# Nested products for six of the seven products of q, v and k in a float32 attention and non-local block

## The chip, the cores and the metric

The kernel runs on one core of a Trainium2 chip. The metric is the device time of one execution in microseconds (us), lower is better. TensorE (PE) multiplies matrices, VectorE (DVE), ScalarE (ACT) and GpSimd (POOL) work element by element, SyncE (SP) issues most DMAs. All data is float32.

## The reference, cut to what matters

Eight images of 512 channels and 32 x 32 positions pass through two layers:

```
h, d = 8, 64                                  # 8 heads of 64 channels, n = 1024 positions
q, k, v = (conv1x1(x, W, b) for q, k and v)   # 512 -> 512 channels each
attn = softmax(einsum('bhdn,bhdm->bhnm', q, k) * d ** -0.5)
x = x + conv1x1(einsum('bhnm,bhdm->bhdn', attn, v), Wp, bp)

g, theta, phi = (conv1x1(x, w, b) for g, theta and phi)   # 512 -> 256 channels
f = einsum('bcn,bdn->bcd', theta, phi) / n
z = conv1x1(einsum('bcd,bdn->bcn', f, g), W_w, W_b) + x
out = batch_norm(z) over (image, position), times gamma, plus beta
```

The change concerns the three 512 x 512 by 512 x 1024 products that make q, k and v of each image.

## The kernel before, in words

The kernel goes through the images one after the other. For image b it has q, k and v already; it then does, in this order on TensorE: the attention of b (`attention`, 64 steps of scores, exponential and weighted sum); q, v and k of image b+1 (`heads_of`, `values`, `heads_of`), with the softmax denominators of b inside the q stage; the output projection (`project`); theta and phi (`theta_phi`); f, g and z (`nonlocal_`). The order of TensorE's instructions, and of those passed through `pe(...)`, `dve(...)` and `sp(...)`, is kept as written; the rest is placed by a scheduler, which also inserts the waits.

Every large product is made by a scheme of seven block products instead of eight (`SEVEN`, lines 235 to 238; a Strassen-Winograd form). The weight matrix is cut into 2 x 2 blocks of 256 x 256, the data into 2 x 2 blocks of 256 channels by 512 positions. Four sums of weight blocks (`weight_sums`) and four sums of data blocks (`t1` to `t4`, `more_sums`, L216) are formed; seven products are made in PSUM, and each is added to one or two quarters of the result: the first time by ScalarE with the bias (L410, L403, L429), later by VectorE (L346, L430). A block product is 4 matmuls of 128x512 for q and k (8 of 128x256 for v, whose result has positions on partitions).

For q, v and k three of the seven block products (`INNER`, numbers 1, 2 and 6) are made by the same scheme once more, from blocks of 128 x 128 and 128 x 256 (`nested`, L268 and L271): seven matmuls of 128x256 in place of four of 128x512, or fourteen of 128x128 in place of eight of 128x256. They need three more weight sums per product (kept in DRAM beside the weights) and four more data sums (`inner_parts`, L228). `seven` interleaves them with the four plain products by the tables `HALVES`, `STEPS` and `READS`; `fills` are calls that stand at given places in that order, for example sums for the next stages. The projection of images 1 to 6 has two nested products, all others are plain.

Buffers: a weight matrix with all its sums is one tile of 18.5 KB per partition in a pool of two (`wr`); `load_w` (L133) fetches the next one when a stage has ended. A ring of ten 4 KB tiles (`block`, pool `ring`) holds the exponentials and the data sums. PSUM is four slots of two banks, handed from stage to stage in the list `free`.

The softmax denominators: VectorE adds the exponentials of a unit (two heads, half the positions) in `acc` (L466, L468). At the unit's end `together` (L495 to L498) folds the 128 partitions of `acc` to 32: SyncE copies the first quarter, then three GpSimd-issued DMAs add the others, one after the other. In the q stage of the next image, at unit 14 of the interleaving, `all_denominators` makes their sum on TensorE (L525), VectorE takes the reciprocal (L536), and a DMA through DRAM spreads it over partitions (`r`, L582). GpSimd multiplies `o` by it in the v stage (`normalize`, L568, four products of 128x1024).

`near_end` (L884) forms the first data sums of the next image on VectorE at step 62 of 64 of the attention: two of 128x1024 and four of 128x256, ahead of the last sum into `acc`.

At the start, image 0's q, k and v are made with weights that arrive piece by piece (L356 to L369, L852 to L876). Image 0's v has three nested products, its q and k none. At the end, `last_z`, `begin` and `finish` (L818 to L846) form z of the last images, the mean and the variance, and write the output channel block by channel block; a check of the denominators (L986 to L990) stands beside it.

Of the kernel before, what the change touches and what calls it, by code (L numbers as in the profile page):

```python
# [16 lines left out]
P = 128  # L17
# [13 lines left out]
def unshifted(ctx: ExitStack, tc: tile.TileContext, a: dict, out: bass.AP):  # L31
# [19 lines left out]
    wr = ctx.enter_context(tc.tile_pool(name="wr", bufs=2))  # L51
    w3 = ctx.enter_context(tc.tile_pool(name="w3", bufs=3))
    foldp = ctx.enter_context(tc.tile_pool(name="foldp", bufs=1))
    ring = ctx.enter_context(tc.tile_pool(name="ring", bufs=10))
# [47 lines left out]
    def weight_sums(w, a21, which=(3, 4, 5, 6), pin=lambda ins: None):  # L102
        for to, l, r, op in ((3, a21, w[:, 2], ALU.add), (4, w[:, 3], w[:, 0], ALU.subtract),
                             (5, w[:, 0], a21, ALU.subtract), (6, w[:, 1], w[:, 4], ALU.subtract)):
            if to in which:
                pin(nc.vector.tensor_tensor(w[:, to], l, r, op))


    queue = ["WqT", "WkT", "WvT"]
    for b in range(B):  # L110
        queue += (["WqT", "WvT", "WkT"] if b < B - 1 else []) + ["WpT", "tp", "WgT"]
    loaded = []

    INNER = {"WqT": (1, 2, 6), "WkT": (1, 2, 6), "WvT": (1, 2, 6), "WpT": (1, 2)}
    WIDTH = 7 * C + 3 * 3 * P
    rest = {}

    def weights_tile(name, half):
        t = wr.tile([P, WIDTH], F32, tag="w", name=f"w_{name}")
        rest[name] = t[:, 14 * half:]  # L120
        return t, t[:, :14 * half].rearrange("p (i k f) -> p i k f", i=7, k=2)

    def load_w(dma, pin=lambda ins: None):

        if not queue:
            return
        name = queue.pop(0)
        half = quarter(name, 0, 0).shape[2]
        t, w = weights_tile(name, half)
        loaded.append((name, w))  # L130
        if name in kept:
            of = kept["plain"] if name == "WpT" and len(queue) == 2 else kept[name]
            ins = dma.dma_start(t[:, :of.shape[1]], of)  # L133
            pin(ins)
            if len(queue) == 1:
                sp(ins)
            return
        corner[name] = block(f"a21_{name}")[:, :, :half]
        for to, m, k in ((w[:, 0], 0, 0), (w[:, 1], 0, 1), (w[:, 2], 1, 1), (corner[name], 1, 0)):
            dma.dma_start(to, quarter(name, m, k))  # L140

    def weights(name, sums_done=False, pin=lambda ins: None):

        n, w = loaded.pop(0)
        assert n == name
        if name not in kept:
            if not sums_done:
                weight_sums(w, corner[name], pin=pin)
            if name not in ("WqT", "WkT", "WvT"):
                keep("plain" if name == "WpT" else name, w)  # L150
        return w

    def keep(name, w):
        kept[name] = dram.tile([P, 14 * w.shape[3]], F32, tag=f"kept_{name}", name=f"kept_{name}")
        nc.sync.dma_start(kept[name], w.rearrange("p i k f -> p (i k f)"))

    def inner_blocks(w, name, n):

        a = w[:, INNER[name][n]]
        extra = rest[name][:, n * 3 * P:(n + 1) * 3 * P].rearrange("p (i f) -> p i f", i=3)  # L160
        return [a[:, 0, :P], a[:, 1, :P], a[:, 1, P:], a[:, 0, P:], extra[:, 0], extra[:, 1], extra[:, 2]]

    def keep_inner(name, w):

        for n in range(len(INNER[name])):
            inner_weights(name, w, n)
        keep_all(name, w)

    def inner_weights(name, w, n):

        a11, a12, a22, a21, s2, s3, s4 = inner_blocks(w, name, n)
        for to, l, r, op in ((s3, a11, a21, ALU.subtract), (a21, a21, a22, ALU.add), (s2, a21, a11, ALU.subtract),
                             (s4, a12, s2, ALU.subtract)):
            dve(nc.vector.tensor_tensor(to, l, r, op))

    def keep_all(name, w):

        wide = len(INNER[name]) * 3 * P
        kept[name] = dram.tile([P, 14 * w.shape[3] + wide], F32, tag=f"kept_{name}", name=f"kept_{name}")
        nc.sync.dma_start(kept[name][:, :14 * w.shape[3]], w.rearrange("p i k f -> p (i k f)"))  # L180
        nc.sync.dma_start(kept[name][:, 14 * w.shape[3]:], rest[name][:, :wide])
# [49 lines left out]
    def quarters_of(t):  # L231
# [17 lines left out]
    FOUR = tuple((*one[:4], ()) for one in (SEVEN[0], SEVEN[1], SEVEN[2], FIVE[4]))  # L249
    HALVES = ((0, 0), (0, 1), (1, 0), (2, 0), (2, 1), (1, 1), (3, 0), (3, 1))  # L250
    STEPS = {2: [0] * 4 + [1] * 14, 3: [0, 0, 0, 1, 1, 2, 2, 2, 2, 2, 2, 2, 2, 1, 1, 1]}
    READS = {3: ((0, "11", True),), 9: ((0, "12", True),), 11: ((1, "22", True),), 13: ((1, "12", False),),
             15: ((0, "22", False), (0, "21", False))}

    def nested(name, stage, w, data, tags, first, add, positions_out=False):

        slots = [bank(tag, f"{name}_in_{tag}") for tag in tags]
        goes_to = {1: ("11", "21", False), 6: ("12", "22", False), 2: ("21", "t4", True)}
# [23 lines left out]
    def seven(name, w, data, positions_out, first, add, between=None, early=False,  # L282
# [19 lines left out]
        for n, m in HALVES if three else ((n, None) for n in range(len(products))):  # L302
# [16 lines left out]
            for i, (to_ps, at, lhsT, rhs, k) in enumerate(work):  # L319
# [3 lines left out]
                if three and positions_out and not i % 2:  # L323
                    continue
# [879 lines left out]
```

## Time and profile before

| | |
|---|---|
| time of the runs, median of 3 | 2135.36 us (2135.02 to 2135.43) |
| time of the profiled execution | 2134.36 us |
| its span, first to last instruction | 2132.6 us |
| granted TensorE clock, mean | 0.996 |
| TensorE busy | 2108.4 us, 99% |
| VectorE, ScalarE, GpSimd busy | 1390.1, 747.5, 210.3 us |
| HBM read and written | 146.23 and 46.86 MB |
| weights of one matrix, W_q with its sums | 2368 KB, 8.9 us from issue to landing |

The profile's page gives busy times by engine, groups of instructions by line and tile, and the chain of work that ended last, followed back from the last instruction: the engine and line that was late at each moment. Timelines list an engine's instructions with their start, their length, and in brackets the idle time ahead and what ended it. "L468" is a line of the kernel; "acc<-acc,e" are the tiles written and read.

One image takes 261.5 us. Counted from the start of the attention of image 1 (341.0), its parts begin at: q of image 2 451.1, v 475.3, k 498.5, projection 521.3, theta and phi 544.5, g 568.7, f 577.3, z 590.4, next attention 602.5.

### The profile page before, as it was taken

Reading aid. Unit: us, or ns where it says so; the run is one execution under the profiler, and the core shown is the slowest. Engines: PE = TensorE matmul, PEld = TensorE weight load, DVE = VectorE, ACT = ScalarE, POOL = GpSimd, SP = SyncE. Lnnn points to the kernel's source line nnn. Section 1 sums busy time; section 2 is a strip of 40 time slices with the busy share of each in tenths; the row PEclk is TensorE's granted clock in tenths of the full one; section 3 lists DMA queues with packets and bytes.
Section 4 is the critical chain, followed back from the end, with each engine's and each line's share of the span. In section 5 each row is a group of like instructions: output and inputs, shape, how many; then the busy total and the mean of one; then the engine's idle time right before and its main releaser. Section 6 shows DMA issues by size and latency. Waiting matters only on the chain.

```text
span 2132.6 us, 31250 instructions
## 1 busy us (share of the span) xinstructions
PE 2108.4 (99%) x13018; PEld 1124.3 (53%) x13018; DVE 1390.1 (65%) x1856; ACT 747.5 (35%) x873; POOL 210.3 (10%) x221
## 2 busy tenths in 40 slices
PE   9999999999999999999999999999999999999996
PEld 4534764357733567336673366633766347643462
DVE  6566667676576665766657667576674675656746
ACT  1464104641046310463105621066212652056116
POOL 0011100111001110011001120011200111011000
PEclk9999999999999999999999999999999999999998
DMA  6522544224142332423223242242434224122758
GB/s 209 193 41 35 155 160 139 40 36 155 73 142 40 52 135 77 142 40 72 112 111 112 40 102 94 101 107 41 104 129 173 38 39 131 58 55 40 227 200 343
DMA packets 53317, 228.75 MB, mean 107 GB/s; under 512 B 10672, under 2 KB 17328, under 8 KB 45616
## 3 DMA queue, kind: packets, MB, share of 16 engines
q1 hardware_dynamic: 42240, 200.33, 26.9%
q0 software_dynamic: 9072, 24.78, 9.6%
q8 instruction: 104, 1.70, 0.3%
q10 hardware_dynamic: 1856, 1.56, 0.3%
q14 instruction: 45, 0.37, 0.1%
HBM read 146.23 MB, written 46.86 MB: 91 GB/s over the span
## 4 chain that ended last, share of the span: by engine, by line
PE 97%; ACT 1%; DVE 1%; DMA 1%; issue 0%; SPq 0%; DVEq 0%; ACTq 0%
PE po L485 21%; PE ps L459 21%; PE ptp L320 9%; PE pp L320 7%; PE pq L320 6%; PE pk L320 6%; PE pv L320 5%; PE pg L320 4%; PE pv_in_s L268 3%; PE pk_in_s L271 3%; PE pq_in_s L271 3%; PE pz L320 3%; PE pf L670 2%; PE pp_in_s L271 2%; PE pwf L725 1%; ACT z L845 1%
## 5 line engine op out<-in xcount | busy, mean ns | idle before, releaser
L462 ACT ACTIVATE e<-ps 128x1024 f32<-128x1024 f32 x512 | 523.1, 1025 | 436.2 <-PE ps L459 430.0
L468 DVE TENSOR_TENSOR acc<-acc,e 128x1024 f32<-128x1024 f32 x384 | 470.1, 1224 | 145.1 <-ACT e L462 141.9
L459 PE MATMUL ps<-q,k 64*64 64x512 f32 x4096 | 529.6, 590 | 1.0 <-DVE v L430 1.0
L485 PE MATMUL po<-e,v 64*64 64x512 f32 x4096 | 528.7, 589 | 0.0
L485 PEld LDWEIGHTS po<-e,v 64*64 64x64 f32 x4096 | 156.6, 133 | 282.9 <-issue 275.4
L459 PEld LDWEIGHTS ps<-q,k 64*64 64x64 f32 x4096 | 155.4, 133 | 284.6 <-issue 273.4
L498 POOL DMA_DIRECT2D fold<-acc x189 | 144.7, 766 | 1613.8 <-PE ps L459 836.2
L713 ACT ACTIVATE g<-pg,gb 128x512 f32<-128x512 f32 x31 | 21.3, 687 | 475.6 <-PE pg L320 475.5
L466 DVE TENSOR_TENSOR acc<-e,e 128x1024 f32<-128x1024 f32 x64 | 78.3, 1224 | 132.5 <-ACT e L462 132.5
L430 DVE TENSOR_TENSOR v<-v,pv_in_s 128x256 f32<-128x256 f32 x136 | 56.8, 421 | 97.6 <-PE pv_in_s L268 79.4
L320 PE MATMUL ptp<-w_tp,t_x 128*128 128x256 f32 x512 | 114.4, 379 | 0.0
L320 PEld LDWEIGHTS ptp<-w_tp,t_x 128*128 128x128 f32 x512 | 97.3, 190 | 13.2
L320 PE MATMUL pp<-t_o,w_WpT 128*128 128x512 f32 x208 | 100.8, 592 | 0.0
L320 PE MATMUL pq<-t_x,w_WqT 128*128 128x512 f32 x200 | 100.6, 596 | 0.0
L320 PE MATMUL pk<-t_x,w_WkT 128*128 128x512 f32 x200 | 100.0, 592 | 0.0
L320 PE MATMUL pv<-w_WvT,t_x 128*128 128x256 f32 x384 | 98.8, 380 | 0.0
L320 PE MATMUL ptp<-w_tp,x 128*128 128x256 f32 x384 | 86.8, 379 | 0.0
L568 POOL TENSOR_TENSOR o<-o,r 128x1024 f32<-128x1024 f32 x28 | 65.4, 2354 | 153.7 <-DMA r<-den_d 131.5
L320 PEld LDWEIGHTS ptp<-w_tp,x 128*128 128x128 f32 x384 | 73.0, 190 | 13.3 <-issue 3.8
L346 DVE TENSOR_TENSOR k<-k,pk_in_s 128x256 f32<-128x256 f32 x119 | 48.0, 419 | 47.7 <-PE pk_in_s L271 35.1
L346 DVE TENSOR_TENSOR q<-q,pq_in_s 128x256 f32<-128x256 f32 x119 | 48.1, 416 | 45.1 <-PE pq_in_s L271 32.8
L320 PE MATMUL pp<-o,w_WpT 128*128 128x512 f32 x144 | 67.8, 593 | 1.6 <-DVE o L566 1.6
(200 smaller groups left out, 2349.1 us busy)
## 6 DMA issues: line engine op xcount, KB each, us to landing
fold<-acc POOLq DMA_DIRECT2D x189, 128.0 KB, 3.1
w_WqT<-kept_WqT SPq DMA_DIRECT2D x7, 2368.0 KB, 8.9
w_WvT<-kept_WvT SPq DMA_DIRECT2D x7, 2368.0 KB, 8.8
w_WkT<-kept_WkT SPq DMA_DIRECT2D x7, 2368.0 KB, 16.2
r<-den_d SPq DMA_DIRECT2D x32, 512.0 KB, 6.7
x<-in_x_dram SPq DMA_DIRECT2D x30, 512.0 KB, 5.9
w_WpT<-kept_WpT SPq DMA_DIRECT2D x6, 2176.0 KB, 8.1
w_tp<-kept_tp SPq DMA_DIRECT2D x7, 1792.0 KB, 7.2
```

The source lines that it names most:

```text
L268: pe(nc.tensor.matmul(ps[:, i, :], d[di][:, i * P:(i + 1) * P], a[wi], start=s not in begun and not i, stop=True, skip_group_check=True))
L271: pe(nc.tensor.matmul(ps, a[wi], d[di], start=s not in begun, stop=True, skip_group_check=True))
L320: pe(nc.tensor.matmul(to_ps, lhsT(k), rhs(k), start=(s, at) not in begun, stop=(k == nk - 1), skip_group_check=True))
L346: pin(nc.vector.tensor_tensor(at, at, ps if len(ps.shape) == 3 else ps.unsqueeze(1), ALU.add))
L430: lambda q, ps: dve(nc.vector.tensor_tensor(at(q), at(q), as_v(ps), ALU.add)), **how)
L459: pe(nc.tensor.matmul(ps[c * P // 2:(c + 1) * P // 2, j, :], k[r, p, keys], q[r, p, h * 512:(h + 1) * 512], start=True, stop=True, skip_gr ...
L462: nc.scalar.activation(e, ps, AF.Exp, scale=SCALE)
L466: nc.vector.tensor_tensor(accs[u], es[u, 0], e, ALU.add)
L468: ins = nc.vector.tensor_tensor(accs[u], accs[u], e, ALU.add)
L485: pe(nc.tensor.matmul(ps[j * D:(j + 1) * D, r, :], v[keys, m, (2 * p + j) * D:(2 * p + j + 1) * D], e[keys, j, :], start=(m == 0), stop=(m ...
L498: nc.gpsimd.dma_start(to, part_of, accum_op=ALU.add)
L568: dve(nc.gpsimd.tensor_tensor(at, at, of, ALU.mult))
```

## The change

Six of the seven block products of q, v and k are nested, for images 1 to 7; only the product of the blocks 11 stays plain. Image 0's q, k and v are all plain. A new function `six` takes them in three pairs, `SIX`, whose matmuls alternate, over all four PSUM slots. Products that go to several quarters are collected in three temporary tiles (T1, T6, T7 in the pool `w3`) and added to the quarters by GpSimd, for v partly by VectorE. The bias enters by T1 and, as a difference (`dq`, `dk`), by T7.

Weights are held by blocks: units of 7 KB per partition, two nested blocks with their sums each, in a pool of four (`wr`), and the plain first block in a pool of two (`wf0`). `load_w` fetches one unit after each pair. The ring has twelve tiles. To make room, `tpb` is loaded again for every image, `dens` lies in a ring tile that is loaded at the end, `f` in a ring tile, and the sums of `o` in the tile of `fold`. W_k of image 0 lies at first in the tiles of `o` and `fold`.

The denominators and the reciprocal stand at `"middle"`, between the second pair and the plain product of q. Two of the four products with `r` move from GpSimd to VectorE. The data sums of the next image, now four nested blocks more, are formed one by one at the steps `AT` of the attention (26 to 57).

The core of the diff (the rest of it renames, or follows from the blocks):

```diff
-    wr = ctx.enter_context(tc.tile_pool(name="wr", bufs=2))
+    wr = ctx.enter_context(tc.tile_pool(name="wr", bufs=4))
+    wf0 = ctx.enter_context(tc.tile_pool(name="wf0", bufs=2))
-    ring = ctx.enter_context(tc.tile_pool(name="ring", bufs=10))
+    ring = ctx.enter_context(tc.tile_pool(name="ring", bufs=12))
...
+    PAIRS = ((1, 6), (3, 4), (5, 2))
+    UNITS = {"WqT": PAIRS, "WkT": PAIRS, "WvT": PAIRS, "WpT": ((1, 2), (3, 4, 5), (6,)), "tp": ((3, 4, 2), (6, 5, 1)),
+             "WgT": (range(7),)}
...
+    SIX = (((1, "21", "11"), (6, "22", "12")), ((3, "t1", "22"), (4, "t2", "T6")), ((5, "t3", "T7"), (2, "t4", "21")))
+    ORDER = (0, 1, 2, 5, 4, 3, 6)
+
+    def six(name, w, data, positions_out, at, write, fills):
...
+        def add(q, of, engine=None):
+            dve((engine or nc.gpsimd).tensor_tensor(to(q), to(q), to(of), ALU.add))
+
+        def plain():
+            ps = next_bank(f"{name}_0")
...
+            load_w("first")
+            add("T6", "T1", nc.vector if positions_out else nc.gpsimd)
+            if not positions_out:
+                add("11", "T1")
+            add("12", "T6")
+
+        for n, pair in enumerate(SIX):
+            if n == 2:
+                for one in fills.pop("middle", ()):
+                    one()
+                plain()
+            slots = [next_bank(f"{name}_in_{n}_{i}") for i in range(4)]
+            free[:] = [free[2], free[3], free[0], free[1]]
+            begun = set()
+            for step, which in enumerate(ORDER):
+                _, wi, di, chain, reads = SEVEN[which]
+                for m, (outer, of, q) in enumerate(pair):
+                    a, d = w.inner(outer)[wi], data[f"inner {of}"][di]
+                    ps = slots[m if not chain else 2 + m][:, chain // 2, :256]
...
+                        pe(nc.tensor.matmul(ps, a, d, start=start, stop=True, skip_group_check=True))
+                    for (i, j), is_first in reads:
+                        i, j = int(i) - 1, int(j) - 1
+                        if is_first:
+                            write(q, i, piece(q, i, j), ps)
+                        else:
+                            dve(nc.vector.tensor_tensor(piece(q, i, j), piece(q, i, j), ps, ALU.add))
+                for one in fills.pop((n, step), ()):
+                    one()
+            load_w()
+            if n == 1:
+                add("12", "22")
+        assert not fills, fills
+        if positions_out:
+            add("11", "T1", nc.vector)
+        add("T7", "T6")
+        add("22", "T7")
+        add("21", "T7")
...
-            return [lambda k=k, h=h: product(o["o"][:, :, h * 512 + k * 256:h * 512 + (k + 1) * 256], r[:, k, h])
+            return [lambda k=k, h=h: product(o["o"][:, :, h * 512 + k * 256:h * 512 + (k + 1) * 256], r[:, k, h],
+                                            None if k else nc.gpsimd)
...
+    dq, dk = (const.tile([P, CC // 2], F32, tag=n, name=n) for n in ("dq", "dk"))
+    for to, of in ((dq, bq), (dk, bk)):
+        nc.vector.tensor_tensor(to, of[:, CC // 2:], of[:, :CC // 2], ALU.subtract)
+    weight_sums(wk, corner["WkT"], pin=dve)
+    keep_inner(w_first)
...
+    AT = (26, 29, *(33 + 8 * n // 5 for n in range(16)))
...
+            data = nxt["data"]
+            t3, t4 = (inner_one_by_one(data, of) for of in ("t3", "t4"))
+            q = heads_of(b + 1, "q", weights("WqT"), bq, data, dve, steps=dq, fills={
+                (0, 6): [lambda: more_sums(data, (3,), dve)], (1, 0): [lambda: more_sums(data, (4,), dve)],
+                (1, 6): t3[:2],
+                "middle": [lambda: nxt.update(products=normalize(denominators(next_bank(f"den_{b}")))), *t3[2:], *t4]})
+            products = nxt["products"]
+            v = values(b + 1, weights("WvT"), data, fills={(0, 6): products[:2], (1, 6): products[2:]})
+
+            kept_o = foldp.tile([P, 4, N], F32, tag="fold", name=f"t_o_{b}")
+            nxt["o"] = data_sums(quarters_of(o), f"o_{b}", ())
+            nxt["o"].update({f"t{i + 1}": kept_o[:, i, :].rearrange("p (a n) -> p a n", a=2) for i in range(4)})
+            o_sums = [lambda i=i: more_sums(nxt["o"], (i,), dve) for i in range(1, 5)]
             if b:
+                more = inner_one_by_one(nxt["o"], "21")
             else:
+                w_p = loaded[1]
+                more = [lambda i=i: weight_sums(w_p, corner["WpT"], (i,), dve) for i in (3, 4, 5)]
+            k = heads_of(b + 1, "k", weights("WkT"), bk, data, dve, steps=dk, fills={
+                (0, 6): o_sums[:1], (1, 0): o_sums[1:2], (1, 6): o_sums[2:], "middle": more})
             if b:
                 inner_sums(nxt["o"], "t4", dve)
...
+    both = block("sane")
+    dens, sane = both[:, 0, :], both[:, 1, :]
     for to, d in own:
-        nc.sync.dma_start(to, d)
+        nc.sync.dma_start(dens[:, to], d)
     last_z()
```

## The prediction

> **What bounds the kernel now.** I read the page first (busy time, then the chain that ended last), then the chain in order of time to price the stages, then the timelines of GpSimd and VectorE in the stage that changes. The page:
>
> ```profile
> span 2132.6 us, 31250 instructions
> ...
> PE 2108.4 (99%) x13018; PEld 1124.3 (53%) x13018; DVE 1390.1 (65%) x1856; ACT 747.5 (35%) x873; POOL 210.3 (10%) x221
> ...
> PE 97%; ACT 1%; DVE 1%; DMA 1%; issue 0%; SPq 0%; DVEq 0%; ACTq 0%
> ```
>
> TensorE has no holes to close: only less TensorE work shortens this kernel, and every new wait of TensorE lengthens it. The longest pieces of the chain (start, length) price that work:
>
> ```profile
> 29.20 24.03 PE pk L320 x56
> ...
> 451.06 3.63 PE pq L320 x8
> ...
> 475.26 3.45 PE pv L320 x16
> ...
> 498.45 3.44 PE pk L320 x8
> 521.32 4.29 PE pp L320 x10
> 544.53 24.17 PE ptp L320 x112
> ...
> 577.28 6.25 PE pf L670 x56
> ```
>
> A float32 matmul leaves two records, so one of 128x512 costs 24.03/28 = 0.858 us, of 128x256 24.17/56 = 0.432, of 128x128 6.25/28 = 0.223. The q, v and k stages of an image last 24.20, 23.19 and 22.87 us. Worked out, q and k are 16 x 0.858 + 21 x 0.432 = 22.80, v is 32 x 0.432 + 42 x 0.223 = 23.19: v and k have no holes; q holds in addition the denominators (16 records, 1.0 us) and 0.4 us lost around them.
>
> Two things that the change moves hang on other engines. The last row sums of an image reach `fold` by one DMA of SyncE and three of GpSimd, each waiting for the one before (columns: start, length, idle before and its end):
>
> ```profile
> 456.23 0.77 POOL L498 DMA_DIRECT2D fold<-acc  x1 [9.08 <-DVE q L346]
> 459.24 0.77 POOL L498 DMA_DIRECT2D fold<-acc  x1 [2.24 <-DMA fold<-acc]
> 462.58 0.77 POOL L498 DMA_DIRECT2D fold<-acc  x1 [2.58 <-DMA fold<-acc]
> ```
>
> The last lands about 465.6, and the denominators ask for it only at 472.8. And GpSimd computes only in v:
>
> ```profile
> 485.39 9.43 POOL L568 TENSOR_TENSOR o<-o,r 128x1024 f32<-128x1024 f32 x4 [22.04 <-PE pv_in_s L268]
> ```
>
> ```profile
> 488.91 0.80 DVE L430 TENSOR_TENSOR v<-v,pv_in_s 128x256 f32<-128x256 f32 x2 [3.16 <-PE pv_in_s L268]
> ```
>
> ```profile
> L568 POOL TENSOR_TENSOR o<-o,r x28: 2343/2352/2368, 222.5 to 1787.0; 128x1024 f32<-128x1024 f32 x28
> ```
>
> Beside it VectorE does nothing but L430, whose second input is PSUM. In none of the seven images does a VectorE sum of two SBUF tiles lie beside a GpSimd product, so this trace says nothing of that pairing.
>
> [...] the first `fold` transfer of image 0, issued at 91.37 beside 455 GB/s of other traffic, let GpSimd go on at 97.8, against 2.3 us median.
>
> **The change part by part.** All from the profiled execution (2134.36 us, 1.0 below the median of the runs).
>
> *TensorE work.* q and k become 4 x 0.858 + 42 x 0.432 = 21.57 us, v 8 x 0.432 + 84 x 0.223 = 22.19. Gone per image: 1.23 + 1.00 + 1.23 = 3.46 us, and the 0.4 around the denominators, which now stand elsewhere: 3.8. Seven images: 26.8 us. This is all that can be won.
>
> *First v.* Image 0 loses its nested products: 56 x 0.432 = 24.19 against 23.19, +1.0. Its last product is now read by ScalarE alone, so the wait of 1.01 us on v before the third score matmul (79.32) goes. Net 0.
>
> *Reads inside a pair.* A step is two matmuls, 0.86 us; a slot's next product comes 1.29 us after its last ended. A reader starts 0.2 to 0.27 after a matmul's end and takes 0.44 (ScalarE, back to back) or 0.37 (VectorE), so 0.4 us is left; the six ScalarE reads in a row lag by 6 x 0.01. Zero, as long as VectorE is not late by over 0.5 us. At q's start the fourth slot is the last `po` bank, free 1.4 us in, wanted at 1.3: +0.2.
>
> *Denominators.* They move from 21.7 us into q to the end of the second pair, 28 x 0.432 = 12.1. The sums of the next image are spread over earlier steps, so VectorE's last `acc` no longer queues behind 2.6 us of them: the fold chain starts at -0.15 instead of +2.4, and its last piece lands about 12.1, just when wanted. But the first 917 KB weight block is now loaded at 6 us, beside the second GpSimd DMA. Bounds 0 (no slowing) to 3 us; I take 1.2. Behind the waiting matmuls queue the plain product and the third pair; on VectorE the reciprocal and six inner sums. These six (2.1 us) end before the third pair's first read.
>
> *GpSimd sums.* 7 in q, 5 plus 2 products in v, 7 in k: 7 x 2.35 = 16.5 us a stage. They hide behind 22 us unless they block VectorE. In q the six inner sums fall between GpSimd's first sum (ends 15.1) and its second (starts near 17.5): no loss. In v the products on VectorE wait 1.4 us for a GpSimd product, then 2.35 for a sum, and are done 0.3 before they would cost: none. In k: v's last two sums run from 3.4 to 8.1 us, so `t1` and `t2` of o (asked at 5.8) end at 10.4 instead of 8.2, and TensorE waits 0.6. After k's second pair VectorE has `t3`, `t4` (1.2 each) and four inner sums (0.35 each) before its next PSUM read, due 19.4; GpSimd has four sums in the same stretch (one from 12.4, three from 16.4 back to back). If none gets between, the read is on time: 0. If every VectorE sum has to let a GpSimd sum pass, VectorE is free at 25 and TensorE stands 5.6 us. I take the middle, 3.2: one sum of 2.35 beyond the first two. Then k's last three GpSimd sums meet the four inner sums of `t4` ahead of the project stage: 0 to 0.8, taken 0.5.
>
> Per image: -3.8 + 0.2 + 1.2 + 0.6 + 3.2 + 0.5 = +1.9; seven images +13.2.
>
> *Weights in blocks.* A load waits for one pair's slot and has three pairs (18 us) to land; a like one (896 KB, WgT) takes 4.5. Queued on SyncE behind it: the r broadcasts, wanted only in v. The second tp block comes 10 us before use. Nothing. tpb reloaded for each image: 128 KB twice, over 25 us ahead: nothing.
>
> *Start.* In the built order VectorE takes bq and bk differences before the first sum; bk lands at 6.44 + 4.9 = 11.3, against 10.36 when VectorE starts now. Then a sum of WkT stands before `w4` and `t2` and waits for the fourth WkT piece, near 15.6. TensorE, which has no slack there, waits 0.8 + 2.2: +3.0 (0.7 if that piece lands early, 4 if late).
>
> *End.* The check of the denominators moves from a gap of VectorE (2076.9) to between mean and 1/std of the first channel block, 0.4 + 0.7 before and 0.7 after the reciprocal, where ScalarE waits (2083.5 to 2084.5) and then runs without a break: +1.6 (0 to 4 if the loads of `dens`, now last on SyncE before the output, land late).
>
> Sum: 13.2 + 3.0 + 1.6 = +17.8, so 2134.4 + 17.8 = 2152.2, and 1.0 for the median: **2153**.
>
> **Rivals.** *VectorE gets through* (the faster side): the lock doesn't bind these sums[...]. Then k's 0.6, 3.2 and 0.5 go: -2.4 an image, -16.8, and +4.6 for start and end: 2122, median 2123; with no wait for the fold and an easy start 2111. For it: 35% of VectorE is free, and the read slack of 0.5 us holds elsewhere. Against: 16.5 us of GpSimd per stage leave few holes. It decides at about 2 us of waits in k: below that the kernel is faster. *Strict turns*: k's middle costs 5.6, the project stage 0.8: +4.6 an image, 32.2 + 4.6 = 36.8: 2171, median 2172; with a fold wait of 2.5 us, 2181. For it: three GpSimd sums are ready at once. *Fold bound*: no lock, but 3 us of fold wait: -0.6 an image, -4.2 + 4.6: 2135, no change. For it: the chain has no slack left at all.
>
> **How the numbers follow.** Lock in part (my forecast, 2140 to 2162): 0.37. Strict turns (2162 to 2182): 0.21. VectorE gets through (2111 to 2130): 0.33. Fold bound: 0.09, split as 0.08 no change and 0.01 slower. About 0.2% (4.3 us) is what a measurement of this kernel can tell from no change. Faster 0.33, same 0.08, slower 0.59. The range 2115 to 2176 leaves out about a tenth at each end; the forecast's own is 2140 to 2162.
>
> **What would show it.** Right: TensorE idle in k's third pair, before its second read of a slot, ended by DVE; VectorE sums of two SBUF tiles (t_o, i_o) in k longer than 1.22 and 0.42 us, or with gaps in front, while GpSimd runs; GpSimd's at 2.35 or longer. The q stage should last 22.6 plus the fold wait, v 22.2, k 22 plus 4. Wrong: k at 21.6 with t_o at 1.22 beside a running GpSimd sum; or a fold wait over 3 us; or TensorE waiting on ACT inside the pairs, which I price at nothing.

## The result and the profile after

The changed kernel takes 2159.4 us (median of four runs, 2158.65 to 2160.68), the kernel before 2135.4: a ratio of 1.011, 95% interval 1.0093 to 1.0128. It is slower by 24 us. The profiled execution has a span of 2158.1 us against 2132.6. Its page, busy time and chain:

```profile
span 2158.1 us, 33299 instructions
...
PE 2105.4 (98%) x13486; PEld 1175.5 (54%) x13486; DVE 1495.6 (69%) x1935; ACT 844.2 (39%) x1220; POOL 512.2 (24%) x340
...
PE 84%; DVE 9%; DMA 3%; ACT 2%; issue 1%; SPq 0%; ACTq 0%; DVEq 0%; POOLq 0%
```

Before, the chain was TensorE for 97%; now VectorE holds 9% of it and DMA 3%. TensorE has less to do, yet the end comes later, so it must be waiting. The chain in order of time (start, length), from q of image 2 to theta and phi of image 1, shows for whom (the projection that follows q, v and k of an image is that of the image before it):

```profile
463.96 12.49 PE pq_in L418 x56
...
487.78 12.51 PE pv_in L415 x112
...
515.71 3.12 DVE t_o L252
...
526.91 2.45 DVE i_o L264 x3
532.71 7.42 DVE i_t_o L264 x3
...
558.43 24.17 PE ptp L340 x112
```

q and v have shrunk (together from 47.3 to 46.0 us); then VectorE's sums of o come into the chain, and the piece that matters is the last: 7.42 us for three inner sums `i_t_o`, which are 128x256 and last 0.42 us when nothing disturbs them. The fold comes just in time: its last piece in this image is issued here, and the denominators begin at 476.45.

```profile
472.99 0.77 POOL L610 DMA_DIRECT2D fold<-acc  x1 [2.64 <-DMA fold<-acc]
```

Now both engines in one timeline from the end of k into the projection (start, length, engine):

```profile
527.33 2.56 POOL L371 TENSOR_TENSOR T_pk<-T_pk,T_pk 128x1024 f32<-128x1024 f32 x1 [1.87 <-ACT T_pk L512]
...
529.85 5.02 POOL L371 TENSOR_TENSOR k<-k,T_pk 128x1024 f32<-128x1024 f32 x2
...
532.71 2.45 DVE L264 TENSOR_TENSOR i_t_o<-t_o,i_t_o 128x256 f32<-128x256 f32 x1
534.84 2.53 POOL L371 TENSOR_TENSOR T_pk<-T_pk,T_pk 128x1024 f32<-128x1024 f32 x1
535.08 2.56 DVE L264 TENSOR_TENSOR i_t_o<-t_o 128x256 f32<-128x256 f32 x1
...
537.44 4.90 POOL L371 TENSOR_TENSOR k<-k,T_pk 128x1024 f32<-128x1024 f32 x2
537.57 2.56 DVE L264 TENSOR_TENSOR i_t_o<-t_o,i_t_o 128x256 f32<-128x256 f32 x1
540.05 1.40 DVE L730 SCALAR_TENSOR_TENSOR x<-pp,bp,x 128x512 f32<-128x512 f32 x2
...
541.83 0.70 PE L297 MATMUL pp_in_s<-i_o,w_WpT 128*128 128x256 f32 x2 [2.41 <-DVE x L446]
```

Read the two engines against each other. Each of these three `i_t_o` is issued while a GpSimd sum runs and ends about 0.3 us after that sum's end; the next GpSimd sum then goes ahead of the next `i_t_o`. That is taking turns, one whole instruction each: 2.45 to 2.56 us for 0.42 us of work. The waiting is inside the duration of the VectorE instruction, so VectorE looks busy (13.93 of the 14 us from 526 to 540) while it mostly stands. Behind the four inner sums queues L730, the first read of a projection product; TensorE, which needs that bank, stands 2.41 us before 541.83.

A second cost follows the first. The mean granted TensorE clock of the same stretch, from that wait to the end of the projection, in image 1 and in image 3 (columns: length; busy time of PE, PEld, DVE, ACT and POOL; granted clock; DMA share; GB/s):

```profile
541.83:558.30 16.47, 16.47 (x51) 9.63 (x52) 10.29 (x19) 0.00 (x0) 0.51 (x1) 1.00 0.20 55
1066.19:1084.30 18.11, 18.11 (x50) 10.51 (x51) 10.40 (x19) 0.00 (x0) 0.51 (x1) 0.91 0.17 48
```

The instructions are the same, but after an equal wait (six of them, 14.5 us in sum, all 2.41 to 2.42) image 3 is granted 0.91 of the clock and takes 1.64 us longer. This happens in images 3, 5 and 6 and not in 1, 2 and 4.

What tells these images apart can be read from the traces. The clock recorded in after's and before's is either full or half (1.0 or 0.5). After's stretches at half clock begin at 18.37, 301.68, 1066.26, 1591.91, 1844.50 and 2141.46 us, all on one grid with a step of 3.4133 us; the first five last 3.41 us each, one step (in e8 and e9 one lasts 6.8 us), and the end of the run cuts off the last. Laid out on this grid, the wait of image 3 falls into one step, and that of image 1 is parted between two (same columns):

```profile
537.21:540.62 3.41, 2.21 (x7) 0.85 (x5) 3.41 (x3) 0.00 (x0) 3.33 (x3) 1.00 0.21 76
540.62:544.03 3.41, 2.20 (x7) 1.44 (x8) 2.51 (x6) 0.00 (x0) 1.72 (x1) 1.00 0.00 0
1062.85:1066.26 3.41, 0.99 (x4) 0.16 (x2) 3.41 (x5) 0.00 (x0) 3.41 (x2) 1.00 0.00 0
1066.26:1069.67 3.41, 3.41 (x6) 2.08 (x7) 1.18 (x3) 0.00 (x0) 0.44 (x1) 0.50 0.00 0
```

TensorE is idle for 1.20 and 1.21 us of the first two steps and for 2.42 of the third, and only the third is followed by half clock. In the traces of after and before (whose grid is laid out from its one stretch, at 2117.58 us) this parts the steps without exception: of those at full clock, the 7 in which TensorE is idle for 2.08 us or more are followed by a step at half clock, and the 1233 with 1.84 us or less are not. So an equal wait cost more or less here according to where the grid fell, and that differs from run to run (images 3, 5 and 6 here, 1, 2, 4 and 6 in e5). Why the clock falls is not shown.

Ahead of the end there are five steps at half clock, at 18.4, 301.7, 1066.3, 1591.9 and 1844.5 us. TensorE is busy for 16.3 us in them and loses at most half of that, 8.2 us (an estimate from these figures). The last 17 us are at half clock as well, as the last 15 are before, but no matmul runs there. So about a third of the 25 us lost are TensorE running slowly after it has waited.

The account of the +25.5 us, from the first matmul of each stage in the two timelines:

| place | change | of it half clock, at most |
|---|---|---|
| start: k of image 0 at 34.0 instead of 29.0 us, less 0.3 that v of image 0 wins back | +4.7 | 1.5 |
| q, v and k of image 1: q and v 1.6 shorter, k 1.6 longer | 0.0 | 0 |
| theta/phi stage of image 0, 32.4 instead of 24.2 us (12.9 late at its end) | +8.2 | 1.7 |
| projections of images 1 to 6, 160.2 instead of 139.3 us in sum | +20.9 | 4.9 |
| q, v and k of images 2 to 7 | -10.9 | 0 |
| projection, theta and phi of image 7 | +1.2 | 0 |
| end, from the first g product of image 7 | +1.3 | 0 |

In image 0 the second block of theta's and phi's weights came late (chain of waits):

```profile
292.49 6.50 DMA w_tp<-in_WthetaT_dram
299.62 1.23 DVE tp L757
```

It takes the buffer of the projection's blocks 1 and 2, and in image 0 these must first get their inner sums (after the projection, 289.12 to 291.56) and be stored.

### The profile page after: what moved, and what is told of

It reads as the page before. It is cut to its first block, busy times and chain, and to the rows that moved or that the text cites. A ratio compares the mean times of both kernels' runs of the same rounds, so it can differ in the third digit from the quotient of the medians.

```text
span 2158.1 us, 33299 instructions
## 1 busy us (share of the span) xinstructions
PE 2105.4 (98%) x13486; PEld 1175.5 (54%) x13486; DVE 1495.6 (69%) x1935; ACT 844.2 (39%) x1220; POOL 512.2 (24%) x340
## 4 chain that ended last, share of the span: by engine, by line
PE 84%; DVE 9%; DMA 3%; ACT 2%; issue 1%; SPq 0%; ACTq 0%; DVEq 0%; POOLq 0%
PE ps L571 20%; PE po L597 20%; PE ptp L340 8%; PE pv_in L415 6%; PE pq_in L418 5%; PE pp L340 4%; PE pg L340 4%; DVE t_o L252 3%; PE pz L340 3%; DVE i_t_o L264 2%; PE pf L792 2%; PE pp_in_s L297 2%; DVE k L424 1%; PE pv L381 1%; PE pv L340 1%
## 5 line engine op out<-in xcount | busy, mean ns | idle before, releaser
L424 DVE TENSOR_TENSOR v<-v,pv_in 128x256 f32<-128x256 f32 x84 | 34.8, 421 | 51.9 <-PE pv_in L415 50.9
L371 POOL TENSOR_TENSOR k<-k,T_pk 128x1024 f32<-128x1024 f32 x28 | 70.1, 2524 | 0.5
L763 DVE TENSOR_TENSOR tp<-tp,ptp 128x1024 f32<-128x1024 f32 x24 | 29.3, 1221 | 53.5 <-PE ptp L340 53.5
L371 POOL TENSOR_TENSOR q<-q,T_pq 128x1024 f32<-128x1024 f32 x28 | 65.4, 2356 | 0.5
L418 PE MATMUL pk_in<-i_t_x,w_WkT 128*128 128x256 f32 x224 | 57.3, 383 | 2.0 <-DVE k L424 1.2
L510 ACT COPY k<-pk_in 128x256 f32<-128x256 f32 x112 | 42.0, 375 | 44.3 <-PE pk_in L418 40.6
L539 ACT COPY v<-pv_in 128x256 f32<-128x256 f32 x112 | 41.8, 374 | 44.2 <-DVE T_pv L424 19.3
```

The lines of the kernel that those rows point to most:

```text
L371: dve((engine or nc.gpsimd).tensor_tensor(to(q), to(q), to(of), ALU.add))
L418: pe(nc.tensor.matmul(ps, a, d, start=start, stop=True, skip_group_check=True))
L424: dve(nc.vector.tensor_tensor(piece(q, i, j), piece(q, i, j), ps, ALU.add))
```

## The experiments

Stage lengths in us, from first matmul to first matmul, for all kernels: q, v and k of image 2 and the projection of image 1. Times are medians.

| kernel | q | v | k | projection | theta/phi of image 0 | time |
|---|---|---|---|---|---|---|
| before | 24.1 | 23.2 | 22.9 | 23.2 | 24.2 | 2135.4 |
| after | 23.7 | 22.3 | 22.5 | 25.9 | 32.4 | 2159.4 |
| e1_no_k_sums | 23.5 | 22.3 | 22.3 | 23.2 | 32.4 | 2135.7 |
| e2_one_input | 23.6 | 22.3 | 22.5 | 23.2 | 32.5 | 2138.2 |
| e3_t4_later | 23.5 | 22.3 | 22.5 | 23.2 | 32.9 | 2139.1 |
| e4_all_on_vector | 24.3 | 28.9 | 23.3 | 23.4 | 32.2 | 2189.7 |
| e5_start | 23.7 | 22.3 | 22.5 | 27.6 | 32.2 | 2156.1 |
| e6_first_tp_block | 23.6 | 22.3 | 22.5 | 25.9 | 29.0 | 2155.8 |
| e7_denominators_later | 32.1 | 22.3 | 22.5 | 27.6 | 33.7 | 2223.1 |
| e8_four_moves | 23.6 | 22.3 | 22.5 | 23.2 | 30.2 | 2129.6 |
| e9_half_sums | 23.5 | 22.4 | 22.0 | 23.2 | 33.6 | 2133.6 |
| e10_five_moves | 23.6 | 22.3 | 22.5 | 23.2 | 24.2 | 2124.9 |
| e11_moves_and_halves | 23.6 | 22.4 | 22.0 | 23.2 | 24.2 | 2120.5 |
| e12_moves_and_quarters | 23.7 | 24.1 | 22.0 | 23.7 | 24.2 | 2135.4 |

**e1: k without its GpSimd sums.**

```diff
         def add(q, of, engine=None):
+            if name.startswith("pk"):
+                return
             dve(...)
```

> Leaves out the seven GpSimd sums of k (k is then not the reference's); everything else stands, so the time shows what those sums cost. Theory (turns between GpSimd's sums and VectorE's sums with two SBUF inputs): k's stage falls from about 22.45 to 21.6 us and the projection from 25.9 to 23.3 us, 0.9 us in seven images and 2.6 us in six, together 22 us: 2137 us. In the trace t_o and i_t_o are back at 1.22 and 0.42 us each. Rival A (the wait for the fold ahead of the denominators is what costs): q's stage is untouched by this edit, so at most 3 us are gained: 2156 us or more. Rival B (ScalarE's writes between the banks, not GpSimd, hold the pairs and the projection): nothing is gained, 2159 us, with the instructions short but the waits still there.

Measured: 2135.66 us, ratio to before 0.9999 (0.999 to 1.0007): 23.7 us less than after. The projection is back at 23.2. But k itself has gone down by only 0.2 us, from 22.47 to 22.25, not by 0.9. So nearly all that k's sums cost is paid in the projection, not in k; A and B fall as causes of the loss. In k of image 1, where VectorE forms weight sums, 1.8 us go as well (24.4 to 22.6). k does not reach the 21.57 us of its matmuls: of the 0.7 us left, 0.3 stand behind v's last GpSimd sums, which run on into k here too and block a `t_o` (3.12 us), and 0.4 behind ScalarE in the third pair.

**e2: the four sums of t4 with one input.**

```diff
-        return [lambda ...: pin(nc.vector.tensor_tensor(t[:, i], l, r, ALU.subtract))
+        return [lambda ...: pin(nc.vector.tensor_scalar(t[:, i], l, 2.0, 1.0, ALU.mult, ALU.mult))
```

> The four inner sums of t4 of o, which stand between k and the projection, become operations with one SBUF input of the same size (the operand doubled; the projection's result is then not the reference's). All GpSimd sums stay. Theory (what excludes is the second SBUF input of the VectorE sum): the four take about 0.4 us each beside the GpSimd sums, the projection falls from 25.9 to about 23.4 us in six images, 15 us together: 2144 us. Rival A (VectorE and GpSimd share their way to SBUF in any case, the number of inputs doesn't matter): the four still take about 2.5 us, 2159 us. Rival B (fold wait): 2159 us, as in after.

Measured: 2138.22 us, 1.0012 (1.0005 to 1.0019); projection 23.2. The time is lower than I expected, and yet the reason I gave does not hold. The tile's instructions (count, then least, median and most ns):

```profile
L265 DVE TENSOR_SCALAR i_t_o<-t_o x24: 279/1421/2433, 529.8 to 1821.1; 128x256 f32<-128x256 f32 x24
```

In each image the first lasts 0.41 us, the second and third 2.43, the last 0.28, against 0.42 for a sum of the same size: two of the four are held up, though each reads one SBUF tile. So the second SBUF input is not what decides for this operation; why it is held up is not shown. The projection is mended because the four now take 5.3 us and not 8.1, so the first read starts 5.0 us into the projection and not 7.7. What an operation with one input in SBUF and one in PSUM does is told by other lines (L446 in e3, 0.41 us), not by this run.

**e3: the four sums of t4 nine us later.**

```diff
             if b:
-                inner_sums(nxt["o"], "t4", dve)
+                between = {1: lambda: inner_sums(nxt["o"], "t4", dve)}
```

> Only moves the four inner sums of t4 of o: from ahead of the projection to after its second product, about 9 us later, when k's GpSimd sums are over; the projection's nested products need them only some 17 us after it begins. Theory: they take 0.42 us each there, the first read of a projection product is no longer late, and the projection falls from 25.9 to about 23.4 us in six images: 2145 us. Rival A (the projection's own VectorE sums, one input from SBUF and one from PSUM, are excluded too by k's last GpSimd sums): these grow to 2.5 us in their place and the projection stays above 25 us. Rival B (fold wait): nothing changes, 2159 us.

Measured: 2139.12 us, 1.0015 (1.0008 to 1.0022): 20.3 us less than after from moving 24 short instructions. All six projections last 23.2 us. Both engines in the projection:

```profile
537.29 4.67 POOL L371 TENSOR_TENSOR k<-k,T_pk 128x1024 f32<-128x1024 f32 x2
537.57 0.41 DVE L446 TENSOR_TENSOR x<-x,pp_in_s 128x256 f32<-128x256 f32 x1
...
542.62 0.42 DVE L264 TENSOR_TENSOR i_t_o<-t_o 128x256 f32<-128x256 f32 x1
```

L446, with one input in SBUF and one in PSUM, takes its 0.41 us in the middle of two GpSimd sums, so A falls; and the inner sums take 0.42 once GpSimd is done (541.96). It gained more than the 14.5 us that I computed from one projection, because in three images the clock came back as well.

**e4: all sums of the six products on VectorE;** two of the four products with `r` stay on GpSimd.

```diff
-            dve((engine or nc.gpsimd).tensor_tensor(to(q), to(q), to(of), ALU.add))
+            dve(nc.vector.tensor_tensor(to(q), to(q), to(of), ALU.add))
```

> All sums of the six products go to VectorE, in the same places of its order; GpSimd keeps only the o products and the fold. No turn-taking is left in q and k. Theory: an unblocked sum is 1.22 us, 17 of them 20.7 us per image on VectorE, in q (15.1 of 23.8 us busy before) and k (19.9, of which about 4.3 is blocked time) it becomes nearly full, and the last three sums of k and the four of t4 still stand ahead of the projection's first read. What is saved in turns is about lost in length: 2155 us, between 2140 and 2175. If GpSimd's sums cost much more than they relieve, it is under 2140 us; if the rival (turns cost little) holds, it is over 2170 us, since VectorE gets 20 us more per image for nothing.

Measured: 2189.73 us, 1.0252 (1.0235 to 1.0269), 30 us over after and outside what I gave. By my own bound this would have spoken for the rival, that turns cost little. The trace says otherwise: the projection lasts 23.4 us, q and k of image 2 lose 0.6 and 0.8 us, and v loses 6.6. There q's last sums, now on VectorE, meet the two o products that stayed on GpSimd:

```profile
492.84 6.18 POOL L677 TENSOR_TENSOR o<-o,r 128x1024 f32<-128x1024 f32 x2 [15.29 <-DMA r<-den_d]
...
493.57 6.54 DVE L371 TENSOR_TENSOR q<-q,T_pq 128x1024 f32<-128x1024 f32 x2
...
500.49 2.08 PE L415 MATMUL pv_in<-w_WvT,x 128*128 128x128 f32 x8 [3.83 <-DVE v L424]
```

Two sums of 1.2 us take 6.54, TensorE stands 3.83 us and then needs 2.08 us for eight matmul records that take 1.05 otherwise. So GpSimd's sums relieve VectorE a little (the 0.6 and 0.8 us of q and k); most of the loss is the same exclusion at another place.

**e5: the start.**

```diff
-        nc.vector.tensor_tensor(to, of[:, CC // 2:], of[:, :CC // 2], ALU.subtract)
+        dve(nc.vector.tensor_tensor(to, of[:, CC // 2:], of[:, :CC // 2], ALU.subtract))
```

> Two small VectorE subtractions (dq and dk, 128x2) are kept in program order, so that they stand behind the first image's sums and not ahead of them; with that the first sum of k's weights also stands behind the sums that image 0's q waits for, as in before. Nothing else moves. Theory: the 2.65 us wait for k's weights and the 0.8 us for the biases leave VectorE's path to q's second and third product, k of image 0 starts at about 29.5 instead of 34.0 us, all later stages keep their lengths: 2155 us. Rival (the first microseconds are bound by the DMA of the first weights, which has more to bring before x's next part): k still starts at 32 us or later, 2157 us or more.

Measured: 2156.12 us, 1.0095 (1.0079 to 1.011). k of image 0 starts at 29.2 us, as in before (29.0): the start is mended in full. The total gains 3.3 us and not 4.8. In the profiled execution four projections (images 1, 2, 4 and 6) went on at half clock after their wait, not three. In e1, e2, e6 and e9, which have the start of after, k begins at 31.7 to 32.0 us: in e9, where it begins at 31.67, TensorE waits 1.97 us in q and not 2.40, and no half clock follows.

**e6: the first block of theta and phi.**

```diff
-"WpT": ((1, 2), (3, 4, 5), (6,))
+"WpT": ((3, 4, 5), (1, 2), (6,))
...
         if b == 0:
+            load_w()
             for i in INNER:
...
-            keep("WpT", w, (0,))
+            keep("WpT", w, (1,))
...
-        load_w(times=3)
+        load_w(times=3 if b else 2)
```

> The projection's second weight block in the buffers becomes the one with the products 3, 4 and 5 and not the one with 1 and 2, so that the second block of theta's and phi's weights takes the buffer of 3, 4 and 5, which is free after the projection's fifth product; its load is issued ahead of the inner sums and stores of the blocks 1 and 2. Theory: in image 0 the load lands before the first product of theta and phi ends, the 8.2 us that TensorE waited from 292 to 301 us go, and only there: 2151 us, and the theta/phi stage of image 0 is about as long as image 1's. Rival (the transfer itself is slow beside the stores and loads around it): 3 us or less are gained and the wait for the same load remains.

Measured: 2155.82 us, 1.0095 (1.008 to 1.0111); the stage falls from 32.4 to 29.0 us, as the rival's number has it. The rival's reason is wrong, though: the load is issued at 275.3 us and its block is summed at 278.8, before the projection ends (285.0). What is late instead is shown under e8, which has the same edit.

**e7: the denominators behind the plain product** (in q alone; the edit is shortened).

```diff
             if n == 2:
-                for one in fills.pop("middle", ()):
-                    one()
                 plain()
+                for one in fills.pop("late"):
+                    one()
```

> The softmax denominators of the image before move from ahead of q's plain product to behind it, with the inner sums that follow them; TensorE has 3.7 us more work before it needs the fold. Everything else as in after. Theory (turns between the engines): the trace shows only 0.3 to 0.4 us of waiting ahead of the denominators in most images, so at most 3 us are gained, 2157 us, and it can be 2 us worse because the reciprocal now stands among the reads of q's third pair: 2157 to 2162 us. Rival (the prediction's own term: the fold lands after the denominators are due, 1.2 us an image): 8 us are gained, 2151 us.

Measured: 2223.07 us, 1.0408 (1.0392 to 1.0424), 64 us over after. Neither theory said so, and the miss teaches most. Beside the denominators the edit moves six inner sums of the data, and these now fall among GpSimd's sums of q:

```profile
492.98 4.99 POOL L371 TENSOR_TENSOR q<-q,T_pq 128x1024 f32<-128x1024 f32 x2
493.22 2.55 DVE L264 TENSOR_TENSOR i_t_x<-t_x,i_t_x 128x256 f32<-128x256 f32 x1
...
495.70 2.56 DVE L264 TENSOR_TENSOR i_t_x<-t_x 128x256 f32<-128x256 f32 x1
...
498.40 2.90 PE L423 MATMUL pq_in<-i_t_x,w_WqT 128*128 128x256 f32 x6 [6.68 <-DVE i_t_x L264]
```

TensorE waits 6.68 us for them, then takes 2.90 us for six matmul records that take 1.5 at full clock (ahead of the end this execution is at half clock for about 75 us, after for 17). q lasts 32.1 us instead of 23.7. In after, the same sums stood in the gap between two GpSimd sums and cost nothing.

**e8: e3, e5 and e6 together, and the loads for the last check earlier.** The end's edit:

```diff
         if last:
+            both = block("sane")
+            held["sane"] = dens, sane = both[:, 0, :], both[:, 1, :]
+            for to, d in own:
+                sp(nc.sync.dma_start(dens[:, to], d))
             take_back(B - LATE)
```

> Computes all of the reference. The edits of e3 (t4's inner sums later), of e5 (start) and of e6 (first theta/phi block) together, and the loads of the old denominators for the last check issued ahead of the last image's g stage, so that the check stands ahead of the last units again and not inside them. Theory: the causes are separate places and add up: 2139.1 of e3, less 5 (start), less 8 (theta/phi block), less 1.4 (end): 2125 us, 0.5% under before. Rival (something else fills the gaps, DMA above all): 2133 us or more.

Measured: 2129.60 us, 0.9971 (0.996 to 0.9983): faster than before. The end is back (80.8 us from the last image's first g product to the last instruction; after 82.1, before 80.7). What is missing to 2125 lies in image 0:

```profile
288.57 1.23 DVE L252 TENSOR_TENSOR t_x<-x,t_x 128x1024 f32<-128x1024 f32 x1
288.68 10.16 PE L340 MATMUL ptp<-w_tp,t_x 128*128 128x256 f32 x32 [2.76 <-DVE t_x L252]
...
294.69 0.42 DVE L107 TENSOR_TENSOR w_WgT<-a_WgT,w_WgT 128x256 f32<-128x256 f32 x1 [2.63 <-DMA w_WgT<-in_WgT_dram]
```

The data sums of theta and phi stand behind the eight inner sums of the projection's weights; TensorE waits 2.76 us for them and then needs 10.16 us for 32 matmul records that took 7.07 before. And a sum of g's weights, waiting for its load, stands ahead of the next reads.

**e9: GpSimd's sums in halves**, on the changed kernel, nothing moved.

```diff
-            dve((engine or nc.gpsimd).tensor_tensor(to(q), to(q), to(of), ALU.add))
+            n = 1 if engine is nc.vector else 2
+            for i in range(n):
+                l, r = (t[:, i * t.shape[1] // n:(i + 1) * t.shape[1] // n] for t in (to(q), to(of)))
+                dve((engine or nc.gpsimd).tensor_tensor(l, l, r, ALU.add))
```

> Each of GpSimd's sums in the six products becomes two of half the size (128x512), one behind the other; nothing else is touched. Theory (VectorE and GpSimd take turns, one whole instruction of the other at a time): a blocked i_t_o lasts one half sum, about 1.3 us and not 2.5, so the projection loses about half of its 2.7 to 4.4 us in six images, about 10 us together, less what two starts cost GpSimd (not known from any trace here): 2149 us, 2145 to 2156. Rival (VectorE waits until GpSimd's queue of ready sums is empty): the blocked time stays the same, 2159 us or more.

Measured: 2133.61 us, 0.9989 (0.998 to 0.9997), 26 us less than after where I expected 10.

```profile
529.41 1.37 DVE L264 TENSOR_TENSOR i_t_o<-t_o,i_t_o 128x256 f32<-128x256 f32 x1
530.71 1.48 DVE L264 TENSOR_TENSOR i_t_o<-t_o 128x256 f32<-128x256 f32 x1
...
532.11 1.48 DVE L264 TENSOR_TENSOR i_t_o<-t_o,i_t_o 128x256 f32<-128x256 f32 x1
533.52 1.40 DVE L733 SCALAR_TENSOR_TENSOR x<-pp,bp,x 128x512 f32<-128x512 f32 x2
```

The turn is as long as one GpSimd instruction: 1.4 us for a half as 2.5 for a whole. For these sums the rival falls. (It doesn't for all: see e12.) My size was wrong because I halved the loss, and a loss is what goes over the slack: the four sums take 5.0 us instead of 8.1, and 3.8 us are free between k and the first read (in e3 VectorE sits idle for 3.81 us there). The first read, 4.6 us into the projection against 3.6 in e3, is still late, but no longer late enough for TensorE to wait: all six projections last 23.2 us, and the half clock behind them goes too. A half costs GpSimd 1.27 us where a whole costs 2.36.

**e10: e8, and in image 0 the data sums ahead of the weights' inner sums.**

```diff
         if b == 0:
             load_w()
+            data = data_sums(quarters_of(xt), f"x1_{b}", (1, 2), pin=dve)
             for i in INNER:
```

> Computes all of the reference. The four moves of e8, and in image 0 the first two data sums of theta and phi are kept ahead of the inner sums of the projection's weights on VectorE, so that TensorE no longer waits for them (2.8 us at 286 us in e8), and with that order g's weight sums are built behind theta's first reads (they held the reads back by 2.6 us in e8). Theory: the theta/phi stage of image 0 falls from 30.2 to about 24.5 us, 2124.5 us in all. Rival (a later load, g's weights or q's, is then late in its turn and takes the time back): 2128 us or more.

Measured: 2124.89 us, 0.9948 (0.9935 to 0.9962), as expected; the stage lasts 24.2 us.

**e11 and e12: the five moves with halves, and with quarters.**

> Computes all of the reference. The five moves of e10 with the halved GpSimd sums of e9. Theory: with the inner sums of t4 already out of the way the halves can only shorten the turns that are left inside q and k, 0.5 us an image (e9's image takes 259.0 us, e3's 259.5): 2124.9 less 3.5, 2121 us. Rival (the halves and the move mend the same wait and no other): 2125 us.

> Computes all of the reference. As e11, but each GpSimd sum in four pieces of 128x256. A half took 1.27 us where a whole took 2.36, so a start costs about 0.1 us; a quarter should take about 0.7 us and a turn cost VectorE 0.7 us. Theory: the turns shrink again, but GpSimd's own work in q, v and k grows by some 7 us an image and its last sums come later: between 2119 and 2126 us, near e11. Rival (the many small turns cost VectorE more than few long ones, since each piece holds it once): 2130 us or more.

e11: 2120.45 us, 0.9928 (0.9915 to 0.9942), 15 us faster than before and the fastest of all; k goes from 22.5 to 22.0 us, as the theory says. e12: 2135.43 us, 0.9999 (0.999 to 1.0007): the rival's side. In v VectorE's two o products take 8.5 us (6.8 in e11), TensorE waits 1.5 and v is 1.7 longer; and the first `i_t_o` of an image waits far longer than one quarter (0.73 us):

```profile
L264 DVE TENSOR_TENSOR i_t_o<-t_o x12: 411/1193/2004, 529.6 to 1827.3; 128x256 f32<-128x256 f32 x12
```

The turn of one instruction is broken already with halves. In e11, v of image 2:

```profile
483.06 4.66 POOL L680 TENSOR_TENSOR o<-o,r 128x1024 f32<-128x1024 f32 x2
485.60 6.80 DVE L680 TENSOR_TENSOR o<-o,r 128x1024 f32<-128x1024 f32 x2
...
487.69 2.48 POOL L374 TENSOR_TENSOR v<-v 128x512 f32<-128x512 f32 x2
```

The first of VectorE's two products lasts 5.66 us: it is issued inside GpSimd's second product and ends 1.1 us after the two halves behind that. In after, with whole sums, none of the 56 VectorE instructions that last over 0.2 us longer beside a GpSimd instruction than they do without waits for more than one. In v of image 2 the first product of e11 waits for three in a row, and that of e12 for six: it is issued at 485.71 inside the first of GpSimd's two products and ends behind the four quarters that follow them (the two take 8.54 us). In e12 the first `i_t_o` of image 1 waits for three quarters, 1.99 us, and six of the twelve in the line above last as long. Why is not shown.

## Why the prediction was right or wrong

The forecast was 2153, "lock in part", and 2159.4 came. Its side and its mechanism hold; the mechanism, the "lock" by which sums of VectorE and GpSimd wait for each other, was the author's assumption, since before holds no such pair, and after shows it (2.45 to 2.56 us for 0.42). That its sum is near is in part luck: one term was some 3 us an image too high, the next as much too low, and two causes were missed.

- *TensorE work*, -3.8 us an image. Right: v lasts 22.3 us (predicted 22.19), and with the lock's cost moved out of the way (e11) q, v, k and projection together last 91.1 us instead of 93.4. The missing 1.5 us are mostly in the next two points.
- *Reads inside a pair*, priced at zero. Somewhat wrong: TensorE waits on ScalarE inside the third pair, which the prediction had named as a sign against it. In k of image 2 this costs 0.4 us (the eight records beside this weight load take 2.28 us instead of 1.89), in e1 and e11 as in after, and it is why k is not under 21.95 us in any kernel. q's first two pairs take 12.5 us instead of 12.1.

```profile
527.30 1.16 PEld L418 LDWEIGHTS pk_in<-i_t_x,w_WkT 128*128 128x128 f32 x6 [0.52 <-ACT T_pk L512]
```

- *Denominators*, 1.2. The fold's end was placed rightly (12.1 us into q; the denominators begin at 12.5). In images 3 to 6 their weight load waits 0.3 us, for a VectorE read and not for the fold; q of images 2 and 7 is 0.3 and 0.8 us longer than theirs. "Fold bound" has no support: q is not shorter in any kernel that leaves the fold as it is, and e7, which gave it time, was slower for another reason.
- *k's t1 and t2 of o and its middle*, 0.6 + 3.2. Here the working failed. The exclusion is there (`t_o` 3.12 and 3.37 us, one `i_o` 2.58), but it takes from VectorE's slack. In image 2 the first term costs 0.3 us (the third pair begins 15.82 us into k, 15.53 in e11) and the middle 0.2 (from there to the projection 6.65 us, 6.44 in e1). GpSimd's sums begin where I had put them (522.5 and 527.3), but three of VectorE's four inner sums fall into the 1.9 us of gap between the first and the second; only the last has to wait, and VectorE is free at 530.17, some 0.7 us late and not 3.2. Only image 1, with its longer weight sums, comes nearer (1.8 us, e1).
- *Project stage*, 0.5 with bounds of 0 to 0.8, counted in seven images though only six have it. This is the term that was mis-sized most: 20.9 us in six images, 3.5 an image, of which 2.7 without half clock. GpSimd's five sums from 529.85 on run back to back until 542.3 us, so there is no gap to slip through; four short sums under strict turns take 8.1 us against a slack of 3.8 (of the 4.3 over, TensorE, with other products in hand, stands 2.4). The upper bound should have been four turns less the slack, as I did reckon for k's middle, and not 0.8. k's two terms and the projection together were given 4.3 us an image and cost 4.0.
- *Weights in blocks*, "Nothing". Wrong by 8.2 us: I counted when the block is wanted, not whose buffer it takes. In image 0 that buffer is held by weights that are still summed and stored; another buffer gives 3.4 us back (e6). The rest is the place of these inner sums on VectorE, ahead of the data sums, and the half clock that follows (e8, e10).
- *Start*, +3.0 with 0.7 to 4: k of image 0 is 5.0 us late, and 2.6 to 3.0 in e1, e2, e6 and e9 (in e9 the clock stays full there). Mechanism right (e5); the clock was not in the sum.
- *End*, +1.6: +1.3. Right (e8 has it back). *First v*, 0: -0.3. Right.

None of the terms held the granted clock. It is up to 8 of the 25 us: each wait of TensorE was priced at its own length, and some were followed by a loss of 1.5 to 1.7 us more. Of the rivals, "Strict turns" had the rule of turns right and the place wrong; "VectorE gets through" is wrong for the turns and right for k, where waits under the slack cost little.

## What to carry to other kernels

When work goes to GpSimd, list every VectorE instruction with two SBUF inputs that can fall beside it (a tensor_scalar with one was held up as well, 2.43 us in e2), and price each at one whole GpSimd instruction (here 2.45 to 2.56 us for 0.42; beside halves and quarters one waited for three and for six); then ask what is next on VectorE's queue and how much slack it has. Moving a few short sums away from GpSimd's, or cutting GpSimd's instructions in two, can be worth more than the change itself: here it turned 24 us lost into 15 us won. A wait of TensorE can bring a second loss, the half clock: here waits of 2.4 us did so in three of six projections, for 1.5 to 1.7 us more. When a fill or a load moves, everything that moves with it counts, and for a buffer its last user.

## What the runs showed of the hardware

- VectorE's sums of two SBUF tiles and GpSimd's sums waited for the whole of each other: a 0.42 us VectorE sum lasts 2.45 to 2.56 us beside GpSimd sums of 2.36, and 1.37 to 1.48 beside halves of 1.27 (after, e9); GpSimd's `v<-v`, issued inside a VectorE product, lasts 3.33 to 3.37 us instead of 2.36 (after). With whole sums they took strict turns: none of the 56 instructions held up in after waited for more than one. With halves and quarters one waited for three and for six (e11, e12). The time waited is within the instruction's duration, so the engine counts as busy (13.93 of the 14 us from 526 to 540 in after).
- A float32 tensor_scalar of 128x256 takes 0.28 us on VectorE and is held up as well (2.43 us, e2). An instruction with one SBUF and one PSUM input is not: 0.41 us for L446 beside two GpSimd sums (e3), 0.40 to 0.43 us for all 264 of 128x256 that lie beside GpSimd instructions in after.
- The recorded clock is 1.0 or 0.5. In after and before all 7 steps of the 3.413 us grid at full clock with TensorE idle for 2.08 us or more were followed by half clock, none of the 1233 with 1.84 us or less. After waits of 2.41 to 2.42 us this came in three of six projections of after, which last 27.4 to 27.6 us instead of 25.9: 1.5 to 1.7 us more. After a wait of 2.76 us, with 6.8 us at half clock, 32 matmul records took 10.16 us instead of 7.07, 3.1 more (e8). The ends of matmuls are modelled in these traces, so the idle times are approximate.
- GpSimd's float32 sum takes 2.36, 1.26 and 0.73 us for 1024, 512 and 256 elements a partition (after, e11, e12): about 0.17 us of it is fixed, an estimate from the first two.
